# One table for every place of the order in a one-core message-passing kernel, with the steps cut into single products, turns and half runs

## The chip, the cores and the metric

The kernel runs on one core of one Trainium2 chip. The metric is the device time of one execution in microseconds. Three executions of the kernel before took 503.43, 501.66 and 503.40 us, median 503.4.

## The reference

128 graphs of 64 nodes with 128 features get one message layer. For every pair (i, j) of nodes of a graph a two-hidden-layer MLP with layer norms makes a message; the adjacency matrix keeps the messages of real edges alone, and their sum per node goes through a second MLP.

```python
f_i, f_j = broadcast(x, i), broadcast(x, j)                  # (B, N, N, C), B=128, N=64, C=128
h = relu(concat([f_i, f_j], -1) @ msg_w0 + msg_b0); h = layernorm(h)
h = relu(h @ msg_w1 + msg_b1);                      h = layernorm(h)
messages = (h @ msg_w2 + msg_b2) * adj[..., None]
agg = sum(messages, axis=2)
updated = x + mlp(concat([x, agg], -1), upd_w0, ..., upd_b2)  # the same MLP with other weights
```

About one pair in eight is an edge, so the kernel computes messages for edges alone: each graph gets 640 edge slots. (A slow path for graphs with more edges stands at the program's end and is not entered.)

## The kernel before, in words

Two graphs make a pair `p` (64 pairs). Edges are worked on in *chunks* of 512 slots: 4 tiles of 128 edges. Five chunks cover four graphs, and there are 160 chunks. A chunk passes through these steps, each a small function:

- `marks` / `compare` (TensorE `mk`, VectorE `j`) and `node_rows` / `stack` (`i`, and the DMAs on SyncE's queue that put `i` and `j` together in `s`): build one-hot matrices `s` that say which two nodes an edge slot has.
- `gather` (TensorE, into the one PSUM bank `hps`): first layer of the MLP as products of `s` with the nodes' precomputed rows. Rows are kept as a low and a high part, `abl` and `abh`, so each piece of a chunk is a pair of products. Because a graph has 640 slots and a chunk 512, the pieces of five successive chunks are 512; 384+128; 256+256; 384+128; 512 columns wide.
- `relu0` (ScalarE, `h`), `turn_h` (four TensorE transposes by `ident` into the one PSUM bank `hT`), `stats0` (two VectorE statistics of `hT`), and some chunks later `seed` (bias into a `z` bank by ScalarE, or into `u` by GpSimd), `layer1` (four products into one of two banks `z0`, `z1`, from `h` itself), `relu1` (`y`; VectorE for half of the chunks, ScalarE for the others), `stats1`.
- `weights` (GpSimd, `w`) and `reduce` (TensorE, 32-column products into `ys`): the masked sums per node.
- For each block of eight graphs the update MLP: `turn` (transposes), `layer_a`, `layer_b`, `layer_c` (products), `layer_out`, `finish` and the store of `uo`.

A product of two float32 operands stands in the profile as two instructions, a transpose and a gather product as one.

The order on each engine is the order in which the steps are called. Each step is entered with `at(n, place, fn, ...)`: `n` is the chunk step and `place` one of 16 places within a chunk step, worked through in a fixed order; a table `MOVE` shifts single steps to another chunk step, place and rank. The table repeats for every tenth chunk in the steady part (about 29 us), and is written out for the start and the end. `keep_busy(k)` issues products into `ys` that nobody reads: `k` products of 128 columns for k over 4, else `k/2` of 256 columns. The table had moved four of these groups from the start to chunk steps 16 and 20.

Of the kernel before, what the change touches and what calls it, by code (L numbers as in the profile page):

```python
# [23 lines left out]
MOVE = {  # L24
# [335 lines left out]
def tile_gnn(  # L360
# [293 lines left out]
    def edge_path(es):  # L654
# [30 lines left out]
        def zbank(k):  # L685
            return ps_z[k].tile([P, CH * C], F32, name=f"z{k}")


        plan = {}
        early_keys = []  # L690

        def at(n, place, fn, *args):
# [955 lines left out]
```

## Time and profile before

| what | value |
|---|---|
| times of three runs | 501.66, 503.40, 503.43 us |
| span of the profiled execution (its own time, first to last instruction) | 501.7 us |
| busy TensorE products / weight loads | 491.1 us (98%) / 467.9 us (93%) |
| busy VectorE | 460.5 us (92%) |
| busy ScalarE | 397.9 us (79%) |
| busy GpSimd | 353.8 us (71%) |
| granted TensorE clock, mean | 0.998 |
| DMA: moved, share of 16 engines on the main queue | 63.55 MB, 58.7% |

Busy time is the union of an engine's instructions. For TensorE it says little: products are pipelined and their ends are modelled, so two products that overlap in the table may still follow each other slowly or quickly. The pace is read from where instructions *start*. The page's chain of work is empty for this run.

### The profile page before, as it was taken

The page shows a single profiled execution, that of the slowest core. Times are in us where ns is not written, and L with a number is a line of the kernel's source. Part 1 is how long each engine was busy: PE and PEld are TensorE (multiplying, and loading weights), DVE is VectorE, ACT ScalarE, POOL GpSimd, SP SyncE. Part 2 cuts the span into 40 slices and gives each one's busy share as a digit, 9 for nine tenths or more (in the row PEclk, how much of TensorE's full clock was granted, in tenths as well). Part 3 has the DMA queues.
Part 4 walks back from the last instruction along what each step waited for, and adds up shares of the span by engine and source line. Part 5 has one row for each costly group of instructions (what it writes and reads, how often), then busy time and mean ns, then how long its engine had stood idle before and what let it go on. Part 6 is the DMA issues. An engine that isn't in the chain of part 4 may idle for free.

```text
span 501.7 us, 15934 instructions
## 1 busy us (share of the span) xinstructions
PE 491.1 (98%) x5969; PEld 467.9 (93%) x5969; DVE 460.5 (92%) x1225; ACT 397.9 (79%) x907; POOL 353.8 (71%) x563
## 2 busy tenths in 40 slices
PE   8899999999999999999999999999999999999995
PEld 5799999999999999999999999999999999999984
DVE  7899789899999999998999999899999989998885
ACT  6999978889787788978778797877879778867753
POOL 3267686877869687786968768696886679674941
PEclk9999999999999999999999999999999999999999
DMA  4668565566948576684857757475564647345201
GB/s 122 157 138 170 122 129 130 114 133 137 164 104 153 126 141 131 130 161 107 160 128 113 157 121 162 104 171 123 121 154 111 156 107 171 88 113 107 63 23 46
DMA packets 91474, 63.55 MB, mean 127 GB/s; under 512 B 57473, under 2 KB 75522, under 8 KB 91394
## 3 DMA queue, kind: packets, MB, share of 16 engines
q1 hardware_dynamic: 91106, 62.36, 58.7%
q8 instruction: 49, 0.80, 0.7%
q14 instruction: 31, 0.25, 0.2%
q10 hardware_dynamic: 288, 0.13, 0.1%
HBM read 7.15 MB, written 4.19 MB: 23 GB/s over the span
## 4 chain that ended last, share of the span: by engine, by line


## 5 line engine op out<-in xcount | busy, mean ns | idle before, releaser
L1003 PE MATMUL z<-w1c,h 128*128 128x128 f32 x1280 | 167.4, 275 | 0.0
L1003 PEld LDWEIGHTS z<-w1c,h 128*128 128x128 f32 x1280 | 158.1, 192 | 4.1
L613 DVE BATCH_NORM_STATS2 st<-hT 128x6 f32<-128x256 f32 x320 | 120.3, 417 | 21.9 <-PE hT L956 18.7
L951 ACT ACTIVATE h<-hps,b0c 128x512 f32<-128x512 f32 x160 | 109.5, 684 | 24.3 <-PE hps L946 23.0
L993 ACT ACTIVATE z<-b1b,m_sd 128x128 f32<-128x128 f32 x320 | 118.8, 371 | 11.6 <-DVE y L597 4.6
L613 DVE BATCH_NORM_STATS2 st<-y 128x6 f32<-128x256 f32 x320 | 117.9, 417 | 0.1
L989 POOL TENSOR_TENSOR u<-b1b,m_sd 128x512 f32<-128x512 f32 x80 | 82.7, 1042 | 29.8 <-ACT m_sd L621 20.2
L956 PE MATMUL hT<-ident,h 128*128 128x128 f32 x640 | 96.6, 273 | 0.7 <-ACT h L951 0.7
L946 PE MATMUL hps<-s,abl 128*128 128x512 f32 (+3 forms) x256 | 93.4, 370 | 1.0 <-DMA s<-j 0.7
L1045 POOL TENSOR_TENSOR w<-oh,m_q 128x192 f32<-128x192 f16 x126 | 62.5, 509 | 39.9 <-issue 27.1
L956 PEld LDWEIGHTS hT<-ident,h 128*128 128x128 f32 x640 | 74.3, 141 | 1.9 <-ACT h L951 1.0
L946 PE MATMUL hps<-s,abh 128*128 128x512 f32 (+3 forms) x256 | 74.4, 322 | 0.0
L1012 ACT ACTIVATE y<-z 128x512 f32<-128x512 f32 x80 | 47.3, 594 | 30.9 <-PE z L1003 30.8
L928 DVE TENSOR_TENSOR j<-mk,cmpt 128x320 fp32r<-128x320 f32 x124 | 58.3, 470 | 1.4 <-PE mk L920 1.2
L597 DVE CUSTOM_DVE_ANT_0 y<-z,u 128x512 f32<-128x512 f32 x80 | 53.9, 674 | 3.9 <-PE z L1003 2.4
L889 ACT ACTIVATE d<-slot,mid 128x640 f16<-128x640 f16 x64 | 52.7, 826 | 0.7 <-DVE mid L799 0.7
L946 PEld LDWEIGHTS hps<-s,abl 128*128 128x128 f32 x256 | 48.7, 190 | 2.9 <-DMA s<-j 0.9
L946 PEld LDWEIGHTS hps<-s,abh 128*128 128x128 f32 x256 | 48.5, 189 | 0.0
L1060 PE MATMUL ys<-y,w 128*32 128x128 f32 x1488 | 44.3, 274 | 0.0
L1060 PEld LDWEIGHTS ys<-y,w 128*32 128x32 f32 x1488 | 39.7, 110 | 3.6 <-POOL w L1045 2.6
L904 POOL CAST i<-tp 128x640 fp32r<-128x640 f16 x58 | 42.4, 745 | 0.0
L920 PE MATMUL mk<-tp,posall 128*128 128x320 f16 x126 | 38.0, 302 | 0.2 <-DVE j L928 0.2
(195 smaller groups left out, 852.2 us busy)
## 6 DMA issues: line engine op xcount, KB each, us to landing
s<-i SPq DMA_DIRECT2D x124, 160.0 KB, 3.0
s<-j SPq DMA_DIRECT2D x124, 160.0 KB, 2.7
xn<-in_x_dram SPq DMA_DIRECT2D x15, 256.0 KB, 3.8
out_dram<-uo SPq DMA_DIRECT2D x15, 256.0 KB, 2.5
an<-in_adj_dram SPq DMA_DIRECT2D x16, 128.0 KB, 2.8
oh<-tp SPq DMA_TRANSPOSE x64, 3.2
xn<-in_x_dram SPq DMA_DIRECT2D x2, 128.0 KB, 2.8
out_dram<-uo SPq DMA_DIRECT2D x2, 128.0 KB, 3.6
```

Source lines behind the costliest of these rows:

```text
L597: nc.vector._custom_dve(TENSOR_ADD_SAT, out=o, in0=ps, in1=sb, s0=BIG, s1=0.0)
L613: nc.vector.bn_stats(st, src.rearrange("p t c -> p c t"))
L889: nc.scalar.activation(D[p], slot, AF.Abs, bias=blocks[b]["mid"][:, q:q + 1], scale=-1.0)
L928: nc.vector.tensor_tensor(JR[p][:, c], MK.pop((p, k))[:, 0:HC], cmpt[:, c], op=ALU.is_equal)
L946: nc.tensor.matmul(ps[:, c:c + w], lhsT=ab[:, g % 4, :], rhs=s, start=(k == 0), stop=(k == 1))
L951: nc.scalar.activation(H[n], HP.pop(n), AF.Relu, bias=b0c)
L956: nc.tensor.transpose(ps[:, t, :], H[n][:, t * P:(t + 1) * P], ident)
L989: nc.gpsimd.tensor_tensor(U[n], bc(W["b1b"], CH), SR[q][:, k:k + CH].unsqueeze(2).to_broadcast([P, CH, C]), op=ALU.mult)
L993: nc.scalar.activation(z_of(n)[:, t, :], W["b1b"], AF.Copy, scale=SR[q][:, k + t:k + t + 1])
L1003: nc.tensor.matmul(ps[:, t, :], lhsT=h[:, t * P:(t + 1) * P], rhs=W["w1c"], start=added and t == 0, stop=True, skip_group_check=True)
L1045: (nc.vector if p == NP - 2 else nc.gpsimd).tensor_tensor(WT[p][:, g], oh, qs, op=ALU.mult)
L1060: nc.tensor.matmul(YS[b][g * N + m * HN:g * N + (m + 1) * HN, k, :], lhsT=w[:, g, m, u, :], rhs=y, start=(u == 0), stop=(u == TH - 1), til ...
```

## The change

The steps are cut finer, so that each can stand anywhere: `gather` issues one product (piece `j`, part `k`) where it issued all pairs of a chunk; `turn_h` one transpose where it issued four; `layer1` two products; `stats0` and `stats1` one statistic each (half a chunk); the update's `turn` and `layer_*` two of four blocks; `layer_out`'s statistics become steps of their own; `stack` one DMA of two; `seed` one of four tiles. The places and the table `MOVE` are gone. A table `WHEN` gives each step a time in 1/144 of a chunk step, and all steps are sorted by it. Four of the seven groups of `keep_busy` products at the start are no longer entered (7 products of 128 columns, and 1, 1 and 2 of 256 columns). Apart from these, each engine has the same instructions as before, in the same shapes and numbers.

```diff
-MOVE = {
-    "gather@1": (-1, "b", 0), "gather@2": (1, "e", -1), "gather@3": (2, "L0", 4),
...
+SCALE = 144
+WHEN = {
+    "gather.0.0": {0: -178, 1: -188, 2: 76, 3: 267, 4: 227, 5: 127, 6: 5, 7: -110, 8: -233,
...
+        def at(n, tag, fn, *args):
+            v = args[0] if args else 0
+            v = v.b if isinstance(v, Unit) else v
+            t = WHEN.get(f"{fn.__name__}{tag}", {}).get(n % 10 if 14 <= n < 138 else 100 + v, 0)
+            plan.append((SCALE * n + t, len(plan), fn, args))
...
-        def stack(p, half, src):
+        def stack(p, half, g):
...
-        def gather(n):
+        def gather(n, j, k):
-            ps = HP[n] = ps_h.tile([P, CH * P], F32, name="hps")
-            for g, e, c, w in sorted(pieces(n), key=lambda v: -v[3]):
-                s = S[g // 2][:, g % 2, e:e + w]
-                for k, ab in enumerate(blocks[g // (2 * PB)]["ab", g // 4 % 2]):
-                    nc.tensor.matmul(ps[:, c:c + w], lhsT=ab[:, g % 4, :], rhs=s,
-                                     start=(k == 0), stop=(k == 1))
+            if n not in HP:
+                HP[n] = ps_h.tile([P, CH * P], F32, name="hps")
+            g, e, c, w = sorted(pieces(n), key=lambda v: -v[3])[j]
+            nc.tensor.matmul(HP[n][:, c:c + w], lhsT=blocks[g // (2 * PB)]["ab", g // 4 % 2][k][:, g % 4, :],
+                             rhs=S[g // 2][:, g % 2, e:e + w], start=(k == 0), stop=(k == 1))
...
-        def turn_h(n):
+        def turn_h(n, t):
...
-        def layer1(n):
+        def layer1(n, t0):
...
-        early(keep_busy, 7)
-        early(keep_busy, 2)
-        early(keep_busy, 2)
-        early(keep_busy, 4)
...
+        for _, _, fn, args in sorted(plan, key=lambda v: v[:2]):
+            fn(*args)
```

What the table does to the order is seen in the built programs. The first place is TensorE in the steady part, around a chunk of 384+128 columns. Before, the four gather products stand together and the four transposes of the chunk ahead (`hT`) behind them:

```order
L920 MATMUL mk_3638<-tp_3345,posall_141 128x320
L946 MATMUL hps_3642<-s_3270,abl_3094 128x384
L946 MATMUL hps_3642<-s_3270,abh_3095 128x384
L946 MATMUL hps_3642<-s_3270,abl_3094 128x128
L946 MATMUL hps_3642<-s_3270,abh_3095 128x128
L956 MATMUL hT_3647<-ident_132,h_3582 128x128 x4
L1003 MATMUL z0_3667<-w1c_357,h_3196 128x128 x4
```

After, at the same place:

```order
L934 MATMUL hps_3616<-s_3318,abl_3063 128x384
L934 MATMUL hps_3616<-s_3318,abh_3064 128x384
L944 MATMUL hT_3621<-ident_132,h_3514 128x128 x2
L934 MATMUL hps_3616<-s_3318,abl_3063 128x128
L944 MATMUL hT_3621<-ident_132,h_3514 128x128
L934 MATMUL hps_3616<-s_3318,abh_3064 128x128
L944 MATMUL hT_3621<-ident_132,h_3514 128x128
L987 MATMUL z0_3650<-w1c_348,h_3191 128x128 x2
```

Each 128-column gather product now has a transpose right behind it. Over the whole program, of the 128 such products 19 were followed by a transpose before, 64 by another of their own kind, and 45 by a float32 product (`z`, an update layer, an unread one, or one that derives a weight); after, 113 are followed by a transpose, 14 by a `marks` product (`mk`) and 1 by its own kind.

The second place is TensorE some 60 us into the run, where the largest group of unread products stood. Before:

```order
L946 MATMUL hps<-s,abh 128x384
L946 MATMUL hps<-s,abl 128x128
L946 MATMUL hps<-s,abh 128x128
L1326 MATMUL ys<-mean_m 128x128 x7
L1003 MATMUL z_1161<-w1c,h 128x128 x4
L920 LDWEIGHTS posall
L920 MATMUL mk<-tp,posall 128x320
L956 MATMUL hT<-ident,h 128x128 x4
L832 MATMUL ma<-ident,xn 128x128 x4
```

After, the same chunk, up to the same four transposes of `xn`:

```order
L934 MATMUL hps<-s,abh 128x384
L934 MATMUL hps<-s,abl 128x128
L944 MATMUL hT<-ident,h 128x128 x2
L934 MATMUL hps<-s,abh 128x128
L944 MATMUL hT<-ident,h 128x128 x2
L987 MATMUL z_1157<-w1c,h 128x128 x2
L820 MATMUL ma<-ident,xn 128x128 x4
```

The seven unread products are gone, and `hT`'s transposes stand between the gather products.

The third place is TensorE near the end, where the last two update units (half blocks, banks `z_...`) and the block ahead of them (bank `mu`) share the engine. Before:

```order
L1109 MATMUL ma<-ident,uh 128x128 x4
L1123 MATMUL z_9219<-u0a,xnT 128x128
L1123 MATMUL z_9219<-w2u,ysumT 128x128
L1123 MATMUL z_9219<-u0a,xnT 128x128
L1123 MATMUL z_9219<-w2u,ysumT 128x128
L1123 MATMUL mu<-u1c,uhT 128x128 x4
L1109 MATMUL hT<-ident,ysum 128x128 x2
L1109 MATMUL hps<-ident,uh 128x128 x2
L1123 MATMUL z_9262<-u0a,xnT 128x128
```

After:

```order
L1095 MATMUL ma<-ident,uh 128x128 x4
L1112 MATMUL z_9211<-u0a,xnT 128x128
L1112 MATMUL z_9211<-w2u,ysumT 128x128
L1112 MATMUL z_9211<-u0a,xnT 128x128
L1112 MATMUL z_9211<-w2u,ysumT 128x128
L1095 MATMUL hT<-ident,ysum 128x128 x2
L1112 MATMUL mu<-u1c,uhT 128x128 x4
L1095 MATMUL hps<-ident,uh 128x128 x2
L1112 MATMUL z_9248<-u0a,xnT 128x128
```

The last unit's two transposes of `ysum` now stand ahead of the four `mu` products instead of behind them.

More of the change, by code (lines that the diff above doesn't have):

```diff
@@ L1012, in relu1, with stats1 @@
                 nc.scalar.activation(Y[n], ps, AF.Relu)
[L1014 removed]
+        def stats1(n, t):
             q, c = divmod(n, QC)
[L1016 removed]
+            if q not in ST1:
                 ST1[q] = stp.tile([P, QT // 2, 6], F32, name="st1", bufs=2)
[L1018 to L1019 removed]
+            two_stats(ST1[q][:, (CH * c + t) // 2, :], Y[n][:, t:t + 2, :])
         def var1_step(q):
@@ L1104, in residual, with turn @@
                                     op=ALU.add)
-        def turn(u, src):
-            u.ps = u.turns()
-            for q in range(u.n):
+        def turn(u, src, q0):
+            if q0 == 0:
+                u.ps = u.turns()
+            for q in range(q0, q0 + 2):
                 nc.tensor.transpose(u.ps[:, q * P:(q + 1) * P], getattr(u, src)[:, q, :], ident)
@@ L1114, in turn_out, with layer @@
             nc.scalar.copy(getattr(u, src + "T"), u.ps[:, 0:u.n * P])
-        def layer(u, *pairs):
-            ps = u.bank()
-            for q in range(u.n):
+        def layer(u, q0, *pairs):
+            if q0 == 0:
+                u.l = u.bank()
+                u.l_ps = u.l[:, 0:u.n * P].rearrange("p (q c) -> p q c", q=u.n)
+            ps = u.l
+            for q in range(q0, q0 + 2):
                 s = slice(q * P, (q + 1) * P)
@@ L1124, in layer, with layer_a, layer_b, layer_c @@
                                      stop=(n == len(pairs) - 1))
-            u.l_ps = ps[:, 0:u.n * P].rearrange("p (q c) -> p q c", q=u.n)
-        def layer_a(u):
-            layer(u, ("xn", u0a), ("ysumT", W["w2u"]))
-        def layer_b(u):
-            layer(u, ("uhT", W["u1c"]))
-        def layer_c(u):
-            layer(u, ("uyT", W["u2c"]))
+        def layer_a(u, q0):
+            layer(u, q0, ("xn", u0a), ("ysumT", W["w2u"]))
+        def layer_b(u, q0):
+            layer(u, q0, ("uhT", W["u1c"]))
+        def layer_c(u, q0):
+            layer(u, q0, ("uyT", W["u2c"]))
         def layer_out(u, o, bias):
@@ L1193, in edge_path @@
                 (1, 1, 2, 2, 3, 3, 4, 4, 4, 5, 5, 6, 6, 6, 7))
+        for b in range(2):
+            blocks[b]["an"] = an0[b]
+            blocks[b]["xn"] = xn0[b]
         for b in range(NB):
@@ L1241, in edge_path @@
-                at(n + t[6], "a", turn_out, u, "uh")
-                at(n + t[7], "a", upd_root0, u)
+                v = u.tag
+                at(n + m0_at, v, bias0, u)
+                at(n + xo_at, v, residual, u)
+                at(n + t[0], v, sums_out, u)
+                halves = range(0, u.n, 2)
+                for q0 in halves:
+                    at(n + t[1], f"{v}.ysum.{q0}", turn, u, "ysum", q0)
+                at(n + t[2], v + ".ysum", turn_out, u, "ysum")
+                for q0 in halves:
+                    at(n + t[3], f"{v}.{q0}", layer_a, u, q0)
@@ L1243, in edge_path @@
+                at(n + t[4], v + ".uh", layer_out, u, "uh", "m0")
+                for q0 in halves:
+                    at(n + t[4], f"{v}.uh.{q0}", layer_stats, u, "uh", q0)
+                for q0 in halves:
+                    at(n + t[5], f"{v}.uh.{q0}", turn, u, "uh", q0)
+                at(n + t[6], v + ".uh", turn_out, u, "uh")
+                at(n + t[7], v, upd_root0, u)
                 if t is STEADY:
-                    at(n + t[7], "e", upd_shift, u, 0, PB)
+                    at(n + t[7], v, upd_shift, u, 0, PB)
@@ L1255, in edge_path @@
-                at(n + t[13], "x", layer_c, u)
-                at(n + t[14], "e" if b == NB - 3 else "m", finish, u)
+                    for q0 in halves:
+                        at(n + t[7], f"{v}.{q0}", upd_shift, u, q0, q0 + 2)
+                for q0 in halves:
+                    at(n + t[8], f"{v}.{q0}", layer_b, u, q0)
+                at(n + t[9], v + ".uy", layer_out, u, "uy", "usdb")
+                for q0 in halves:
+                    at(n + t[9], f"{v}.uy.{q0}", layer_stats, u, "uy", q0)
@@ L1257, in edge_path @@
+                at(n + t[9], v, upd_m1, u)
+                for q0 in halves:
+                    at(n + t[10], f"{v}.uy.{q0}", turn, u, "uy", q0)
+                at(n + t[11], v + ".uy", turn_out, u, "uy")
+                at(n + t[12], v, upd_root1, u)
+                at(n + t[12], v, upd_inverse, u)
+                for q0 in halves:
+                    at(n + t[13], f"{v}.{q0}", layer_c, u, q0)
+                at(n + t[14], v, finish, u)
         for p in range(NP):
@@ L1260, in edge_path @@
                 if p > 2:
-                    at(max(n - 7, p - 2), "x" if p == PB + 1 else "a", distance, p)
-                    at(max(n - 6, p - 2), "m", make_tp, p)
-                at(n - 5, "x" if p == PB else "a", node_rows, p)
-                at(n - 4, "a", stack, p, 0, IR)
+                    at(max(n - 7, p - 2), "", distance, p)
+                    at(max(n - 6, p - 2), "", make_tp, p)
+                at(n - 5, "", node_rows, p)
+                for g in range(2):
+                    at(n - 4, f".0.{g}", stack, p, 0, g)
                 for k in range(2):
-                    at(n - 5 + k, "k", marks, p, k)
-                    at(n - 5 + k, "k", compare, p, k)
-                at(n - 3, "a", stack, p, 1, JR)
+                    at(n - 5 + k, f".{k}", marks, p, k)
+                    at(n - 5 + k, f".{k}", compare, p, k)
+                for g in range(2):
+                    at(n - 3, f".1.{g}", stack, p, 1, g)
             w = p // 2 * QC + QC + L1 + p % 2
             last = p // 2 == NQ - 1
-            at(w - 4, "a", node_marks, p)
+            at(w - 4, "", node_marks, p)
             q, h = divmod(p, 2)
@@ L1284, in edge_path @@
             end = q * QC + QC + L1
-            at(3 if q == 0 else n, "s" if last else "x" if q == 0 else "e0", var0_of, q)
-            at(*((n, "e0") if last else (n + 1, "b")), root_of, q)
-            at(end - last, "e1", var1_step, q)
+            at(n if last else n + 1, "", root_of, q)
+            at(end - last, "", var1_step, q)
             wait = 0 if last else 2
-            at(end + wait, "x" if q == NQ - 2 else "a", root1_of, q)
-            at(end + wait, "x" if q == NQ - 2 else "m", inverse_of, q)
+            at(end + wait, "", root1_of, q)
+            at(end + wait, "", inverse_of, q)
         def by_vector(n):
@@ L1370, in edge_path @@
-        early(place_rest)
-        early(rows, 0, 0, 0, 2)
-        early(keep_busy, 4)
-        early(rows_hi, 0, 0, 0, 2)
-        early(rows_lo, 0, 0, 0, 2)
-        early(marks_here, 0)
-        early(rows, 0, 0, 2, 4)
-        early(keep_busy, 2)
-        early(rows_here, 0, 0)
-        early(rows_here, 0, 1)
-        early(compare_here, 0, 0)
-        early(distance, 1)
-        early(gather, 0)
-        early(relu0, 0)
-        early(keep_busy, 4)
-        early(compare_here, 0, 1)
-        early(make_tp, 1)
@@ new lines, in edge_path @@
+        early(".0", degrees, 0)
+        early("", place_first)
+        early(".0", distance, 0)
+        early(".0", place_pair, 0)
+        early(".0", make_tp, 0)
+        early("", place_rest)
+        early(".0.0.0.2", rows, 0, 0, 0, 2)
+        early(".3", keep_busy, 4)
+        early(".0.0.0.2", rows_hi, 0, 0, 0, 2)
+        early(".0.0.0.2", rows_lo, 0, 0, 0, 2)
+        early(".0", marks_here, 0)
+        early(".0.0.2.4", rows, 0, 0, 2, 4)
+        early(".0.0", rows_here, 0, 0)
+        early(".0.1", rows_here, 0, 1)
@@ new lines, in edge_path @@
+        early(".0.0", compare_here, 0, 0)
+        early(".1", distance, 1)
+        early(".0.0.0", gather, 0, 0, 0)
+        early(".0.0.1", gather, 0, 0, 1)
+        early(".0", relu0, 0)
+        early(".5", keep_busy, 4)
+        early(".0.1", compare_here, 0, 1)
+        early(".1", make_tp, 1)
+        early(".2", distance, 2)
+        early(".1", marks_here, 1)
+        early(".1.0.0", gather, 1, 0, 0)
+        early(".1.0.1", gather, 1, 0, 1)
+        early(".1.1.0", gather, 1, 1, 0)
+        early(".1.1.1", gather, 1, 1, 1)
@@ new lines, in edge_path @@
+        early(".1", relu0, 1)
+        early(".0.0.2.4", rows_hi, 0, 0, 2, 4)
+        early(".1.0", rows_here, 1, 0)
+        early(".1.1", rows_here, 1, 1)
+        early(".1.0", compare_here, 1, 0)
+        early(".0.0.2.4", rows_lo, 0, 0, 2, 4)
+        early(".2.0.0", gather, 2, 0, 0)
+        early(".2.0.1", gather, 2, 0, 1)
+        early(".2.1.0", gather, 2, 1, 0)
+        early(".2.1.1", gather, 2, 1, 1)
+        early(".2", relu0, 2)
+        early(".7", keep_busy, 2)
+        early(".2", make_tp, 2)
@@ L1420, in keep, with empties @@
                 product(W["ps", k])
-            at(n - 1, "x", ahead)
-            at(n, "x", keep)
-            at(n + 1, "m", lambda k=k, empty=empty: empty(W.pop(("ps", k))))
+            def empties(k=k, empty=empty):
+                empty(W.pop(("ps", k)))
+            at(n - 1, f".{k}", ahead)
+            at(n, f".{k}", keep)
+            at(n + 1, f".{k}", empties)
         for n, k in ((2, 2), (3, 2), (4, 2), (5, 2)):
-            at(n, "e", keep_busy, k)
+            at(n, f".n{n}", keep_busy, k)
         fl = const.tile([P, 3], F32, name="fl")
```

406 lines of the change are left out of this document (233 added, 173 removed), and 543 rows, old and new, of tables (MOVE, WHEN).

## The prediction

> **What bounds the kernel now.** I read the page's busy times first, then the busy times by windows, the timelines of TensorE's weight loads and products, the waits, and the DMA issues. The page's first row:
>
> ```profile
> PE 491.1 (98%) x5969; PEld 467.9 (93%) x5969; DVE 460.5 (92%) x1225; ACT 397.9 (79%) x907; POOL 353.8 (71%) x563
> ```
>
> TensorE looks like the bound, VectorE is close behind. The windows (busy time of PE, PEld, DVE, ACT, POOL, granted clock, DMA share, GB/s) say where:
>
> ```profile
> 30.00:40.00 10.00, 10.00 (x108) 9.36 (x107) 9.93 (x24) 9.77 (x27) 6.87 (x11) 1.00 0.83 169
> 48.00:55.00 7.00, 7.00 (x56) 6.64 (x54) 5.92 (x18) 6.77 (x17) 2.89 (x5) 1.00 0.42 97
> 55.00:62.00 7.00, 7.00 (x58) 6.79 (x58) 5.43 (x15) 6.21 (x17) 4.58 (x12) 1.00 0.65 143
> 220.00:225.00 5.00, 5.00 (x44) 4.89 (x43) 5.00 (x14) 3.51 (x9) 3.65 (x5) 1.00 0.58 125
> 250.00:300.00 50.00, 50.00 (x546) 48.77 (x545) 47.34 (x127) 41.02 (x96) 37.11 (x59) 1.00 0.64 130
> 475.00:502.00 27.00, 20.16 (x270) 18.09 (x268) 17.54 (x50) 12.73 (x38) 8.26 (x17) 0.97 0.11 32
> ```
>
> From 30 us on TensorE never pauses; the granted clock is 1.00. VectorE has 2.66 of 50 us free in the steady part, but in places (220 to 225 us) nothing, and in the stretch from 30 to 40 us VectorE and ScalarE are both full. So TensorE sets the time while the order keeps VectorE just inside it. Only from 475 us does TensorE stand idle for long, with a dependent chain of update work.
>
> Busy time does not show TensorE's pace, so I take it from the starts of weight loads (start, length, then the group). A load can run while the product ahead still streams, so I only use distances over whole stretches.
>
> ```profile
> 101.81 0.47 PEld L956 LDWEIGHTS hT<-ident,h 128*128 128x128 f32 x4
> 102.25 0.97 PEld L1003 LDWEIGHTS z<-w1c,h 128*128 128x128 f32 x8
> 103.14 0.19 PEld L946 LDWEIGHTS hps<-s,abl 128*128 128x128 f32 x1
> ...
> 70.69 0.19 PEld L946 LDWEIGHTS hps<-s,abl 128*128 128x128 f32 x1
> 70.86 0.19 PEld L946 LDWEIGHTS hps<-s,abh 128*128 128x128 f32 x1
> 71.00 0.42 PEld L956 LDWEIGHTS hT<-ident,h 128*128 128x128 f32 x4
> 71.38 0.30 PEld L1003 LDWEIGHTS z<-w1c,h 128*128 128x128 f32 x2
> ...
> 105.54 0.19 PEld L946 LDWEIGHTS hps<-s,abh 128*128 128x128 f32 x1
> 105.65 0.30 PEld L1123 LDWEIGHTS mu<-u0a,xnT 128*128 128x128 f32 x2
> 105.87 0.30 PEld L1123 LDWEIGHTS mu<-w2u,ysumT 128*128 128x128 f32 x2
> ```
>
> The first three rows are the scale: a transpose takes (102.25−101.81)/4 = 0.110 us, a record of a float32 product (103.14−102.25)/8 = 0.111. In both lower blocks the `abl`, `abh` named last before the other kind are the 128-column pair. A product's own time shows between the next load and the one after it. With transposes behind the pair, 70.86 to 71.38 is `abl`, `abh` and three transposes: 0.52−0.33 = 0.19 us for the pair. Of this `abl`, with its own kind behind it, has 70.86 to 71.00, 0.14; so `abh`, with a transpose behind it, has 0.05 to 0.06. With float32 products behind the pair, 105.54 to 105.87 is the pair and one record: 0.33−0.11 = 0.22, that is 0.11 each. So a 128-column gather product is short when a transpose follows it and long otherwise.
>
> **The change part by part.** Instructions and shapes are the same apart from the unread products; everything else is place.
>
> *128-column gather products.* The order has 19 pairs whose second product a transpose follows and 45 with a float32 product behind them: 45×0.22+19×0.19 = 13.5 us. After, nearly every product has a transpose behind it; I take 2×0.06 = 0.12 a pair, 64×0.12 = 7.7. That saves 5.8 us. About 59 of the 64 pairs lie after the first 62 us, where TensorE is never idle, and I take 5.3. Bounds: if splitting the pair leaves 0.19 each, 64×0.19 = 12.2 and 1.3 us is saved; if the price does not depend on the neighbour, 0; 5.8 at most.
>
> The Trainium skill, page "TensorE: Matmul & The Clock Gate", section "LDWEIGHTS (loading the stationary operand)", speaks against this term: it gives a load's time as its number of columns divided by 1.2 per ns, the same for every 128-column load, which by estimate is 107 ns. By that, a 128-column product can cost no less than its successor's load, whatever the successor is, and the term would be 0. The transposes and float32 records at 0.11 agree with it, the 0.05 to 0.06 above does not; so I go by the rows and keep the rule's result as a rival.
>
> *Unread products.* The four groups of `keep_busy` that fall out, and what follows each:
>
> ```profile
> 48.73 1.08 PE L1329 MATMUL ys<-first,mean_m 128*128 128x256 f32 x4
> 49.65 0.60 PE L956 MATMUL hT<-ident,h 128*128 128x128 f32 x4
> 50.08 0.60 PE L1329 MATMUL ys<-first,mean_m 128*128 128x256 f32 x2
> 50.52 1.05 PE L1003 MATMUL z<-w1c,h 128*128 128x128 f32 x8
> ...
> 53.87 0.65 PE L1329 MATMUL ys<-first,mean_m 128*128 128x256 f32 x2
> 54.35 0.60 PE L956 MATMUL hT<-ident,h 128*128 128x128 f32 x4
> ...
> 60.31 1.77 PE L1326 MATMUL ys<-mean_m 128*128 128x128 f32 x14
> 61.92 0.50 PE L1003 MATMUL z<-w1c,h 128*128 128x128 f32 x3
> ```
>
> By starts they hold TensorE 0.92+0.44+0.48+1.61 = 3.45 us. Upper bound 3.45. Lower bound 0, since they could stand where TensorE would wait anyway: in 48 to 55 us ScalarE is busy 6.77 of 7.00, so of the three small groups' 1.84 us I take a third, 0.6. In 55 to 62 us VectorE has 1.57 and ScalarE 0.79 us free, and the `z` product behind the last group waits for a bank that ScalarE seeds just before:
>
> ```profile
> 59.11 1.17 ACT L993 ACTIVATE z<-b1b,m_sd 128x128 f32<-128x128 f32 x3
> ```
>
> That bank is ready at 60.3, when the group starts, so the product could have followed at once: I take all 1.6. Sum 2.2, range 0 to 3.45. If the cover is gone, what is late next is `relu0` and the seeds on ScalarE.
>
> *256-column products and the rest of the steady order.* Products followed by their own kind go from 96 to 55 in the order, by float32 products from 0 to 57, by transposes from 30 to 15. Spacing of loads puts 256 columns at about 0.124 us in the first two cases and less with a transpose; so 15 fewer short and 41 fewer own-kind successors nearly cancel. I take 0.4, between a loss of 0.5 and a gain of 1.0, the largest I get by letting the 41 save 0.024 each. The `layer1` halves, `q` and `marks` products keep their prices: 0.
>
> *The transfers.* `stack`'s DMAs now go out one by one on SP's queue, `i` and `j` alternating in halves, ahead of or behind an `xn` load.
>
> ```profile
> PE hps L946 <- DMA s<-j: 0.7, 1, 0.7
> ...
> s<-i SPq DMA_DIRECT2D x124, 160.0 KB, 3.0
> s<-j SPq DMA_DIRECT2D x124, 160.0 KB, 2.7
> ```
>
> Over the whole span TensorE waits once, 0.7 us, for `s`; the transfers land in 3.0 and 2.7 us, about one chunk's time (29.3 us for ten chunks). Cost 0; if that cover goes, one late transfer costs up to 3.0 us, once. I put it in the range only.
>
> *The tail.* The last unit's `ysum` transposes move ahead of four `mu` products:
>
> ```profile
> 487.09 0.35 ACT L1091 COPY ysum<-ys 128x256 f32<-128x256 f32 x1
> 488.32 1.10 PE L1123 MATMUL mu<-u1c,uhT 128*128 128x128 f32 x8
> 489.26 0.38 PE L1109 MATMUL hT<-ident,ysum 128*128 128x128 f32 x2
> 489.70 0.39 PE L1123 MATMUL z<-u0a,xnT 128*128 128x128 f32 x2
> 490.11 0.49 PE L1123 MATMUL z<-w2u,ysumT 128*128 128x128 f32 x2
> ```
>
> `ysum` was ready at 487.44, so the transposes gain 489.26−488.32 = 0.94 us. But the `hps` transposes of `uh` and the product with `xnT` stay behind `mu`; what can be gained is the delay of the product with `ysumT`, 490.11 against 489.70+0.22: 0.2 us, and a little more if ScalarE's copy is better placed. I take 0.3, range 0 to 0.94.
>
> *What is given back.* In the steady part TensorE gains some 5.7 us of 440, 1.3%. VectorE has 5% free on average and none in places, and the one bank `hT` hands work from TensorE to it:
>
> ```profile
> DVE st L613 <- PE hT L956: 18.7, 43, 1.6
> ACT y L1012 <- PE z L1003: 30.8, 44, 1.3
> ```
>
> These waits, 18.7 and 30.8 us in all, are TensorE being the later one; they shrink as it gets faster. They add to more than the gain, so I give back only 0.5 us, range 0 to 4 (half of the gain and more; the second rival).
>
> Sum: 2.2+5.3+0.4+0.3−0.5 = 7.7 us. The profiled execution's span is 501.7, its own time, as the fastest of the three runs (501.66); the other two and the median are 1.7 above it, and nothing in the profile says why. 501.7−7.7 = 494.0 for an execution like the profiled one, 495.7 for one like the others. I predict 495.0, one us of the 1.7 above the sum, and add the same to the cases below.
>
> **The rivals.**
>
> *Slower: spread transposes starve VectorE.* Before, four transposes of a chunk follow each other in 0.44 us. After, gather products, and sometimes `z` products, stand between them, so the last of four comes some 0.5 us later after the first (at the place of the diff's second order, two gather products and their neighbours). VectorE's statistics run in order: a late `hT` holds up everything behind it there (`j`, `y`), and those hold TensorE. VectorE has 2.66 us per 50, 0.156 us per chunk of 2.93 us, to spare, and the gain is 7.7/160 = 0.048 us per chunk. So from 0.20 us of new wait per chunk the kernel is slower; with half of the 0.5 us exposed, 0.25, it loses (0.25−0.156)×160 = 15 us: 501.7+15−7.7+1 = 510. For it: one `hT` bank, 43 waits already. Against it: the statistics are halved as well, so the first half can start after two transposes.
>
> *The cover runs out.* TensorE gets shorter, but VectorE, full in 220 to 225 and in 30 to 40 us, and ScalarE at the start do not; they give back half of the 8.2 that TensorE saves by the terms above: 501.7−4.1+1 = 498.6. For it: the full windows. Against it: the free 5% is four times the gain.
>
> *The price of a 128-column product does not change.* The saving at a transpose is then only a matter of when the load is recorded, and the 5.3 falls out: 501.7−2.4+1 = 500.3. That is also the time that the skill's rule would give. For it: the loads' starts need not be the products' starts. Against it: the lower blocks above compare whole stretches, 0.52 and 0.33 us, and differ.
>
> *More than that.* A new order of every place can also take out idle time at both ends, where TensorE stands 6.8 us in the tail window; with 3.45 for the unread products and 4 us of that: 501.7−(3.45+5.8+0.4+4)+1 = 489.0. For it: idle time is there. Against it: at the end the chain of one unit's steps is as long as before.
>
> **How the numbers follow.** The forecast (gain of 5 to 11 us) has 0.62, the run-out cover 0.17, the unchanged price 0.08, the slower rival 0.07, the further gain 0.06. About 0.5% (2.5 us) is what can be told from no change: faster is below 500.9. The forecast and the further gain are all faster, 0.68; of the run-out cover 0.14, with 0.03 no change; the unchanged price sits 0.6 us inside, so 0.04 each: faster 0.86, no change 0.07, slower 0.07. The forecast's own range is 491 to 498. The range reaches down to 489.5, just short of the further gain, and over the cover and price cases to 500.5, leaving out the slower rival and the edges of both others, about 0.15.
>
> **What the changed kernel's profile would show.** PE records fall from 5969 to about 5947 and no unread products stand after 45 us. The load behind a 128-column gather product followed by a transpose comes about 0.06 us after the one before; at 0.11 the pair term is wrong. Ten chunks take about 28.9 us in place of 29.3. VectorE's busy time stays near 460 us and its share of a 50 us window rises from 47.3 to about 48; VectorE's waits for `hT` fall below 18.7 us (the slower rival: they rise, and TensorE waits for VectorE's `j` or for `hT`'s statistics). PE shows no new waits for `s`. In 48 to 62 us TensorE stays at 14 of 14 busy; a gap there says that the unread products had covered a wait. I am wrong if single banks tie the spread steps more tightly than the waits of before show.

## The result and the profile after

The changed kernel took 535.6 us (median of four runs, 535.2 to 535.9), the kernel before 502.75 us beside it: a ratio of 1.0653, with a 95% interval of 1.0628 to 1.0677. It is 33 us slower, where 495.0 was forecast. The profiled execution spans 533.6 us.

The page's first row and two windows of the changed kernel (PE, PEld, DVE, ACT, POOL busy, granted clock, DMA share, GB/s):

```profile
PE 502.1 (94%) x5947; PEld 461.3 (86%) x5947; DVE 465.2 (87%) x1225; ACT 396.9 (74%) x907; POOL 350.1 (66%) x563
...
48.00:62.00 14.00, 13.31 (x102) 11.51 (x100) 12.05 (x34) 11.60 (x30) 8.18 (x17) 1.00 0.60 139
250.00:300.00 50.00, 47.50 (x630) 44.31 (x630) 44.44 (x116) 37.23 (x82) 35.76 (x54) 1.00 0.60 139
```

TensorE, which never paused in 250 to 300 us before, now stands still for 2.50 of 50 us, and VectorE went from 47.34 to 44.44: no engine is full any more. The work is the same apart from the unread products, so the engines wait for each other. The waits of the changed kernel (engine and line, what it waited for, total us, times, longest us) say where; the last row is what my slower rival would have had to show:

```profile
ACT z L981 <- PE z L987: 36.2, 44, 2.1
PEld z L987 <- ACT z L981: 35.2, 58, 1.3
...
PE z L987 <- ACT z L981: 16.0, 27, 1.0
...
DVE st L630 <- PE hT L944: 20.1, 40, 2.1
```

ScalarE's seeds of a `z` bank wait 36.2 us for TensorE's products in `z`, and TensorE's weight loads wait 35.2 us for the seeds. Before, the waits list has neither: no seed that waits for TensorE and no load or product that waits for a seed. One such place, from the timeline:

```profile
277.38 0.61 PE L987 MATMUL z<-w1c,h 128*128 128x128 f32 x4
277.71 0.47 PEld L944 LDWEIGHTS hT<-ident,h 128*128 128x128 f32 x4
277.82 0.60 PE L944 MATMUL hT<-ident,h 128*128 128x128 f32 x4
278.08 0.37 ACT L981 ACTIVATE z<-b1b,m_sd 128x128 f32<-128x128 f32 x1 [0.60 <-PE z L987]
278.50 0.52 PEld L987 LDWEIGHTS z<-w1c,h 128*128 128x128 f32 x4 [0.32 <-ACT z L981]
278.51 0.71 PE L987 MATMUL z<-w1c,h 128*128 128x128 f32 x4
```

A half of `layer1` runs in a `z` bank; a seed tile of the *same chunk*, meant for the second half, stands behind it in the order and waits until it is done (0.60 us, ended by PE `z`); then the second half waits for that seed. I call this a turn of the bank: it goes from TensorE to ScalarE and back. The tiles are different ones of the bank, but the built program has these waits all the same. The Trainium skill, page "PSUM — Partial Sum Buffer", section "PSUM bank collisions raise a hardware error", tells why: two engines on one bank in the same partitions at once collide even in disjoint columns, so access is guarded by bank and not by address. That these waits are there, the rows show; what would happen without them no run here shows.

The table has it so in three of every ten chunks. In its unit (144 a chunk step) chunk 2 of ten has seed tiles at 695, 709, 710 and **900** with the halves of `layer1` at 794 and 917; chunk 0 has its last seed at 924 between 918 and 926; chunk 4 two seeds at 843 and 850 between 840 and 1065. Before, `layer1` was one step behind all seeds.

A fourth wait in ten chunks is no turn. Here are the other three places of one such stretch (the fourth is the load at 278.50 above), with ScalarE's seeds at the first:

```profile
250.68 0.78 ACT L981 ACTIVATE z<-b1b,m_sd 128x128 f32<-128x128 f32 x2 [0.80 <-PE z L987]
...
251.50 0.52 PEld L987 LDWEIGHTS z<-w1c,h 128*128 128x128 f32 x4 [0.34 <-ACT z L981]
...
253.83 0.52 PEld L987 LDWEIGHTS z<-w1c,h 128*128 128x128 f32 x4 [1.35 <-ACT z L981]
...
273.80 0.30 PEld L987 LDWEIGHTS z<-w1c,h 128*128 128x128 f32 x2 [0.49 <-ACT z L981]
```

By the order of the table, the loads at 251.50, 273.80 and 278.50 are the second halves of chunks 4, 0 and 2 of ten, behind their turns: 0.34+0.49+0.32 = 1.15 us. The longest wait, 1.35 us at 253.83, is the first half of chunk 5. All seeds of its chunk stand ahead of it, and it waits for all four of them though it needs two. Together the four waits are 2.50 us.

To see where the loss lies I take ScalarE's `h` instructions as milestones: one for each chunk, 160 in both kernels. These are those of chunks 80 and 90, counted from 0, before and then after:

```profile
234.97 0.69 ACT L951 ACTIVATE h<-hps,b0c 128x512 f32<-128x512 f32 x1
...
264.41 0.69 ACT L951 ACTIVATE h<-hps,b0c 128x512 f32<-128x512 f32 x1
```

```profile
248.44 0.69 ACT L939 ACTIVATE h<-hps,b0c 128x512 f32<-128x512 f32 x1
...
280.29 0.69 ACT L939 ACTIVATE h<-hps,b0c 128x512 f32<-128x512 f32 x1
```

From chunk 40 to 120, ten chunks take 29.43 us before and 31.84 after, in every stretch within 0.03 us: 2.41 us more, close to the four waits. Chunk 20 is 1.0 us later, chunk 130 25.5 us, the last one 35.2 us, and 3.3 us come back behind it: 31.9 us between the two spans.

### The profile page after: what moved, and what is told of

Same layout as the page of the kernel before. It is cut to its first block, busy times and chain, and to the rows that moved or that the text cites. A ratio compares the mean times of both kernels' runs of the same rounds, so it can differ in the third digit from the quotient of the medians.

```text
span 533.6 us, 15954 instructions
## 1 busy us (share of the span) xinstructions
PE 502.1 (94%) x5947; PEld 461.3 (86%) x5947; DVE 465.2 (87%) x1225; ACT 396.9 (74%) x907; POOL 350.1 (66%) x563
## 4 chain that ended last, share of the span: by engine, by line
## 5 line engine op out<-in xcount | busy, mean ns | idle before, releaser
L987 PE MATMUL z<-w1c,h 128*128 128x128 f32 x1280 | 200.8, 281 | 19.2 <-ACT z L981 16.0
L987 PEld LDWEIGHTS z<-w1c,h 128*128 128x128 f32 x1280 | 173.9, 191 | 41.7 <-ACT z L981 35.2
L981 ACT ACTIVATE z<-b1b,m_sd 128x128 f32<-128x128 f32 x320 | 118.5, 371 | 43.7 <-PE z L987 36.2
L630 DVE BATCH_NORM_STATS2 st<-hT 128x6 f32<-128x256 f32 x320 | 121.7, 418 | 21.2 <-PE hT L944 20.1
L630 DVE BATCH_NORM_STATS2 st<-y 128x6 f32<-128x256 f32 x320 | 123.6, 415 | 0.9 <-ACT y L998 0.8
L944 PE MATMUL hT<-ident,h 128*128 128x128 f32 x640 | 112.5, 278 | 3.0 <-DVE st L630 2.8
L934 PE MATMUL hps<-s,abl 128*128 128x512 f32 (+3 forms) x256 | 98.0, 386 | 0.6 <-ACT h L939 0.5
L934 PE MATMUL hps<-s,abh 128*128 128x512 f32 (+3 forms) x256 | 89.9, 355 | 0.0
L944 PEld LDWEIGHTS hT<-ident,h 128*128 128x128 f32 x640 | 76.4, 141 | 6.3 <-DVE st L630 4.2
L1030 POOL TENSOR_TENSOR w<-oh,m_q 128x192 f32<-128x192 f16 x126 | 64.6, 525 | 18.4 <-DVE m_q L659 14.8
L877 ACT ACTIVATE d<-slot,mid 128x640 f16<-128x640 f16 x64 | 51.0, 818 | 1.0 <-POOL mid L766 0.6
L648 POOL TENSOR_TENSOR m_v<-m_v,st 128x20 f32<-128x20 f32 x31 | 7.2, 231 | 58.6 <-DVE st L630 58.3
```

The costliest lines, as they stand in the source:

```text
L630: nc.vector.bn_stats(st, src.rearrange("p t c -> p c t"))
L877: nc.scalar.activation(D[p], slot, AF.Abs, bias=blocks[b]["mid"][:, q:q + 1], scale=-1.0)
L934: nc.tensor.matmul(HP[n][:, c:c + w], lhsT=blocks[g // (2 * PB)]["ab", g // 4 % 2][k][:, g % 4, :], rhs=S[g // 2][:, g % 2, e:e + w], star ...
L944: nc.tensor.transpose(HT[n][:, t, :], H[n][:, t * P:(t + 1) * P], ident)
L981: nc.scalar.activation(z_of(n)[:, t, :], W["b1b"], AF.Copy, scale=SR[q][:, k:k + 1])
L987: nc.tensor.matmul(ps[:, t, :], lhsT=H[n][:, t * P:(t + 1) * P], rhs=W["w1c"], start=by_vector(n) and t == 0, stop=True, skip_group_check= ...
```

## The experiments

| run | us | ratio to before (95%) | us per ten chunks, 40 to 120 |
|---|---|---|---|
| changed kernel | 535.6 | 1.065 (1.063 to 1.068) | 31.84 |
| e1_seeds_first | 521.3 | 1.037 (1.035 to 1.039) | 30.70 |
| e2_layer1_late | 520.1 | 1.034 (1.033 to 1.036) | 30.64 |
| e3_before_split | 528.1 | 1.050 (1.049 to 1.052) | 31.78 |
| e4_turns_together | 535.9 | 1.066 (1.064 to 1.067) | 31.89 |
| e5_layer1_whole | 517.0 | 1.027 (1.024 to 1.030) | 30.25 |
| e6_pairs_together | 517.8 | 1.029 (1.026 to 1.032) | 30.37 |
| e7_before_no_unread | 501.4 | 0.998 (0.996 to 0.999) | 29.49 |
| e8_late_and_one_whole | 516.7 | 1.026 (1.024 to 1.028) | 30.28 |
| e10_early_and_one_whole | 520.7 | 1.034 (1.032 to 1.036) | 30.61 |
| e3b_before_one_split | 511.4 | 1.018 (1.014 to 1.021) | 30.24 |
| e11_two_whole | 511.4 | 1.016 (1.012 to 1.020) | 29.91 |
| e12_pairs_on_e11 | 512.2 | 1.017 (1.013 to 1.021) | 29.99 |
| e13_tail_whole | 512.6 | 1.019 (1.015 to 1.023) | 29.91 |

The diffs below show the main lines of each change; what a name stands for is said in a comment.

**Is it the turn in the bank?** Two runs take it out of the changed kernel, one by ScalarE's order and one by TensorE's; one puts it into the kernel before; one undoes the rival's cause.

```diff
+        half = {args[0]: t for t, _, fn, args in plan if fn is layer1 and args[1] == 0}
+        plan = [(min(t, half[args[0]] - 1) if fn is seed else t, k, fn, args)   # e1
+                for t, k, fn, args in plan]
```

> The changed kernel, with every tile of a seed placed ahead of its chunk's first layer1 half (only ScalarE's order changes). Theory (a seed tile placed between the two halves of layer1 makes TensorE, ScalarE and TensorE take turns in one z bank, three times in ten chunks): ten chunks fall from 31.85 us to 29.0 to 29.6, the time to 502 to 509 us. Rival (spread transposes starve VectorE): stays within 3 us of 535.6, ten chunks near 31.8.

```diff
+        plan = [(max(t, seeded[args[0]] + 1)       # e2; seeded: time of the chunk's last seed
+                 if fn is layer1 and args[0] in seeded else t, k, fn, args) for t, k, fn, args in plan]
```

> The changed kernel, with the first layer1 half placed behind the chunk's last seed tile (only TensorE's order changes). Theory (turns in one z bank): as when the seeds are moved, ten chunks 29.0 to 29.8 us, 502 to 511 us. If instead ScalarE's order as such costs the time, little comes back: over 525 us. Rival (spread transposes): over 530 us.

```diff
             for t in range(CH):                    # e3, layer1 of the kernel before
+                if t == 2 and 20 <= n < 128 and n % 10 in (0, 2, 4):
+                    seed(n, 3)                     # left out of the seeds ahead
```

> The kernel before, with the last seed tile placed between the two halves of layer1 in the chunks 0, 2 and 4 of every ten from 20 to 127; all else as before. Theory (turns in one z bank, 2.4 us per ten chunks, 33 chunks): 512 to 530 us, ten chunks 30.3 to 31.9 us. Rival (spread transposes): within 3 us of 502.7.

```diff
+        plan = [(turned[args[0]] if fn is turn_h   # e4; turned: time of the chunk's last turn_h
+                 else max(t, turned[args[0]] + 1) if fn is stats0 else t, k, fn, args)
+                for t, k, fn, args in plan]
```

> The changed kernel, with the four transposes of each chunk put together at the place of the last. Theory (turns in one z bank): 533 to 541 us, since the bank's turns stay and the short products behind which a transpose stood are lost. Rival (spread transposes starve VectorE): at most 512 us, and VectorE's waits for hT fall below 18 us.

The turn alone, put into the kernel before in 33 chunks, makes it 25.3 us slower and its ten chunks 31.78 us, as slow as the changed kernel's. Its waits:

```profile
PEld z L1009 <- ACT z L998: 23.1, 33, 1.0
...
PE z L1009 <- ACT z L998: 16.8, 33, 0.8
```

33 waits for 33 turns, 0.70 us of stopped weight loads for each. The rival falls: with the transposes together the time stays (535.9), and VectorE's wait for `hT` is 23.7 us, not less. But removing the turns gave back 14.3 and 15.5 us, not the 25 to 34 expected, and in ten chunks 1.14 and 1.20 us. That is about what TensorE waited behind the three turns of the changed kernel, 1.15 us. So the turn costs time by itself, but in the changed kernel it is half of the loss; that e3_before_split comes out as slow as the changed kernel is a coincidence of sizes. In e3 nothing stands between the two halves and each turn costs its full length, while in the changed kernel other products fill a part of it.

> The kernel before with one turn in a z bank in ten chunks (chunk 2 of ten) in place of three. If each turn has its price by itself: a third of the 25.3 us that three cost, 6 to 11 us more than before. If one turn is absorbed by slack on the other engines and only several together cost: under 3 us.

```diff
-                if t == 2 and 20 <= n < 128 and n % 10 in (0, 2, 4):
+                if t == 2 and 20 <= n < 128 and n % 10 == 2:
```

One turn in ten chunks costs 8.1 us, three 25.3: 0.74 and 0.77 us a turn (11 and 33 turns). Within the spread of the runs they add up, and no slack takes any of it.

**What comes behind it.** With `layer1` late (e2), the loads still wait twice in ten chunks for seeds: 0.90 us for those of chunk 4 and 0.49 us for those of chunk 5.

```diff
+        plan = [(half[args[0]] if fn is layer1 else t, k, fn, args)   # e5; half: time of the later half
+                for t, k, fn, args in plan]
```

> The changed kernel, with both halves of every layer1 together at the place of the later half (TensorE's order alone changes). Theory: with the halves apart, the earlier half stands up to one and a half chunk steps ahead, and TensorE waits there for seeds that ScalarE can't have done yet; together, that wait goes too, and ten chunks fall from 30.7 (seeds ahead of layer1) to 29.2 to 29.6 us, the time to 500 to 508 us. Rival (ScalarE is full in that stretch wherever layer1 stands): ten chunks stay above 30.3 us, 516 to 522 us.

The time, 517.0 us, lies where the rival had it (516 to 522), and the ten chunks, 30.25, just below its 30.3. But the rival's cause is not the one: no wait for seeds is left in the steady part. Other chunks' later `layer1` makes VectorE late in turn, and TensorE waits twice in ten chunks, ahead of `hT` transposes, for VectorE's statistics of the chunk before, as here:

```profile
269.18 0.74 DVE L630 BATCH_NORM_STATS2 st<-hT 128x6 f32<-128x256 f32 x2
...
270.07 0.63 PE L944 MATMUL hT<-ident,h 128*128 128x128 f32 x4 [0.31 <-DVE st L630]
```

So only the chunks with the wait are moved:

```diff
+        late.update({args[0]: t for t, _, fn, args in plan        # e8, on top of e2
+                     if fn is layer1 and args[1] == 2 and args[0] % 10 == 4 and 14 <= args[0] < 128})
```

> The changed kernel with layer1's first half behind the chunk's last seed tile, and in chunks 4 of every ten (halves 1.5 chunk steps apart) both halves together at the later place; the other chunks' halves stay apart. Theory (the steady loss is the z banks' turns in chunks 0, 2 and 4, and the new VectorE waits of the run with whole layer1 came from moving the other chunks' halves): ten chunks 29.1 to 29.6 us, 503 to 508 us. Rival (VectorE's statistics of hT set the pace once the turns are gone): ten chunks stay at 30.2 or more, 515 us or more.

> As the run before, with the seeds of chunks 0 and 2 moved ahead of layer1 in place of layer1 behind them. Theory: the same, 29.1 to 29.7 us per ten chunks, 503 to 509 us. Rival: 30.2 us or more, 515 us or more.

 (its edit is that of e1, with chunk 4's halves together)

Neither theory holds: 30.28 and 30.61 us per ten chunks, 516.7 and 520.7 us, all in the range of the rival. But in the ten chunks of e8 TensorE nowhere waits for VectorE's statistics, as the rival would have it. A single long wait of TensorE is left, for the seeds of chunk 5, which follow the root of a whole group's statistics:

```profile
241.39 0.30 ACT L638 ACTIVATE m_sd<-st,eps_c 128x20 f32<-128x20 f32 x1
241.73 0.78 ACT L981 ACTIVATE z<-b1b,m_sd 128x128 f32<-128x128 f32 x2
242.44 0.67 ACT L939 ACTIVATE h<-hps,b0c 128x512 f32<-128x512 f32 x1
243.01 0.76 ACT L981 ACTIVATE z<-b1b,m_sd 128x128 f32<-128x128 f32 x2
243.83 0.71 PE L987 MATMUL z<-w1c,h 128*128 128x128 f32 x4 [0.59 <-ACT z L981]
```

The two last seed tiles stand behind `relu0`, and the first half of `layer1`, which needs neither, waits for both: the turn's mirror image, with the whole bank waited for again. It is the place of the longest wait of the changed kernel.

```diff
-                     if fn is layer1 and args[1] == 2 and args[0] % 10 == 4 and 14 <= args[0] < 128})
+                     if fn is layer1 and args[1] == 2 and args[0] % 10 in (4, 5) and 14 <= args[0] < 128})
```

> As the run with layer1 late and one chunk's halves together, and the halves of chunk 5 of every ten together at the later place too. That run's trace has one long wait of TensorE left in ten chunks, 0.75 us and 0.10 behind it, for the seeds of chunk 5. If that place is the only one left: ten chunks 29.2 to 29.6 us, 503 to 508 us. If ScalarE and VectorE as a whole are late and the wait only moves on: 30.0 us or more, 513 us or more.

Now 511.4 us and 29.91 per ten chunks, between the two expectations, and TensorE is full again (as the window shows), but the kernel before needs 29.43:

```profile
250.00:300.00 50.00, 49.95 (x540) 47.98 (x539) 47.87 (x125) 40.78 (x94) 36.85 (x60) 1.00 0.58 131
...
240.81 0.19 PEld L934 LDWEIGHTS hps<-s,abl 128*128 128x128 f32 x1 [0.22 <-ACT h L939]
...
241.78 0.14 PEld L944 LDWEIGHTS hT<-ident,h 128*128 128x128 f32 x1 [0.21 <-issue]
```

Two short waits of the loads, 0.22 and 0.21 us, which the kernel before does not have, add up to nearly the 0.48 that remains. That they are its cause is not shown, nor why the issue is late there.

```diff
-                     ... args[0] % 10 in (4, 5) and 14 <= args[0] < 128})
+                     ... (args[0] % 10 in (4, 5) and args[0] >= 14 or args[0] >= 128)})
```

> As the run with two chunks' halves together, and from chunk 128 to the end every layer1 whole at the later half's place. Of that run's 8 us over the kernel before, 6 to 7 arise from chunk 130 to the last relu0, with 1.5 us of TensorE's waits for seeds and 2.5 for hT among them. If the waits for seeds there are the same mechanism and stand alone: 1 to 3 us faster than that run, 508 to 510 us. If VectorE's statistics are late there in any order: no faster, 511 us or more.

No gain (512.6 against 511.4): the loss at the end is not the early half's. That VectorE's statistics are late there, as the second expectation had it, fits and is not shown.

**The two terms of the prediction.**

```diff
+        plan = [(low[args[0]] if fn is gather and args[1:] == (1, 1) and args[0] % 5 in (1, 3)  # low: gather 1, 0
+                 else t, k, fn, args) for t, k, fn, args in plan]
```

> The run with whole layer1, and in addition the second 128-column gather product directly behind the first, where a transpose stood between. If a 128-column product is short with a transpose behind it, net of what the transpose ahead of it loses (0.25 us per ten chunks), this costs 2 to 5 us against the run with whole layer1. If the price doesn't depend on the neighbour: within 1 us of it.

> The run before this one, and in addition the second 128-column gather product directly behind the first, where a transpose stood between. Loads of the earlier pair of runs put the price at 0.20 us of TensorE per ten chunks, 0.41 for the products less 0.21 that the transposes get back: 2 to 4 us slower than the run before this one if TensorE sets the pace there; within 1 us of it if a wait still does.

0.8 us each by the medians, 0.12 and 0.08 per ten chunks. On the kernel with waits left this proved little; on e11, where TensorE is full, it does. The weight loads of the same chunk, first e11, then e12 with the pair together:

```profile
248.64 0.20 PEld L934 LDWEIGHTS hps<-s,abl 128*128 128x128 f32 x1
248.79 0.19 PEld L934 LDWEIGHTS hps<-s,abh 128*128 128x128 f32 x1
248.97 0.32 PEld L944 LDWEIGHTS hT<-ident,h 128*128 128x128 f32 x2
249.26 0.19 PEld L934 LDWEIGHTS hps<-s,abl 128*128 128x128 f32 x1
249.39 0.14 PEld L944 LDWEIGHTS hT<-ident,h 128*128 128x128 f32 x1
249.43 0.21 PEld L934 LDWEIGHTS hps<-s,abh 128*128 128x128 f32 x1
249.59 0.14 PEld L944 LDWEIGHTS hT<-ident,h 128*128 128x128 f32 x1
249.62 0.55 PEld L987 LDWEIGHTS z<-w1c,h 128*128 128x128 f32 x4
250.09 0.25 PEld L1095 LDWEIGHTS ma<-ident,ysum 128*128 128x128 f32 x2
```

```profile
249.57 0.20 PEld L934 LDWEIGHTS hps<-s,abl 128*128 128x128 f32 x1
249.72 0.19 PEld L934 LDWEIGHTS hps<-s,abh 128*128 128x128 f32 x1
249.90 0.32 PEld L944 LDWEIGHTS hT<-ident,h 128*128 128x128 f32 x2
250.18 0.19 PEld L934 LDWEIGHTS hps<-s,abl 128*128 128x128 f32 x1
250.29 0.19 PEld L934 LDWEIGHTS hps<-s,abh 128*128 128x128 f32 x1
250.43 0.20 PEld L944 LDWEIGHTS hT<-ident,h 128*128 128x128 f32 x2
250.60 0.53 PEld L987 LDWEIGHTS z<-w1c,h 128*128 128x128 f32 x4
251.04 0.25 PEld L1095 LDWEIGHTS ma<-ident,ysum 128*128 128x128 f32 x2
```

In e11 the load two behind each 128-column product does come early (249.39 to 249.43 and 249.59 to 249.62, 0.04 us or less; 0.06 was predicted), but the distances around it are longer than 0.11: 0.13 ahead of the first (249.26 to 249.39) and 0.16 between the two (249.43 to 249.59). From the first `abl` to `ma` both hold the same products: 250.09−248.64 = 1.45 and 251.04−249.57 = 1.47 us. The time had moved to the neighbours.

```diff
-        early(keep_busy, 7)      # and likewise the groups 2, 2 and 4 that the change leaves out
+        early(keep_busy, 0)
```

> The kernel before without the four groups of unread products that the change leaves out; nothing else is moved. If they cost what the prediction took, 2.2 us less (500.6); bounds 0 (other engines set the pace there, 502.8) and 3.45 us less (499.4). Slower than before only if the products kept something else in step.

1.5 us less by the medians (0.4 to 2.0 by the ratio's interval). In the trace 0.8 us of the 3.45 come out between chunks 10 and 30, around the places of the groups; the rest went into new waits. (1.3 us more of the difference between the two traces arise before chunk 10, ahead of the groups, and have another source.) From 46 to 60 us TensorE is no longer full:

```profile
46.00:60.00 14.00, 13.03 (x103) 12.05 (x102) 11.42 (x32) 13.08 (x32) 7.48 (x15) 1.00 0.50 115
```

This is the one version faster than the kernel before, by 0.2%, with an interval that ends 0.1% short of no change.

## Why the prediction was wrong

- **The bound** was read rightly: TensorE sets the pace, and the order keeps the others just inside it. I then costed the change by TensorE's own stretches, and took the order of the others as given.
- **The step that failed** is the sentence "The `layer1` halves, `q` and `marks` products keep their prices: 0." The halves' own time did not change, but with a step in halves another engine's step of the same bank comes between, or the early half comes before the bank is ready. In the changed kernel the loads wait 2.50 us per ten chunks for seeds, where 2.41 were lost: 1.15 behind the three turns, and 1.35 at chunk 5, whose first half waits for seeds of the second. With the turns taken out ten chunks go from 31.84 to 30.64, with chunk 4's halves together to 30.28, and with chunk 5's to 29.91. "What is given back", 0.5 us and at most 4, is the term that should have held this. It was to be seen beforehand, in the table and in the order of ScalarE, where a seed follows its own chunk's product. I looked at TensorE's order alone. The prediction's last sign of being wrong, single banks that tie the spread steps more tightly than the waits of before show, is what came.
- **128-column products, 5.3 us:** mis-sized. Between them together and apart lie 0.08 us per ten chunks, about 1 us. The short distance was real, but I took a distance of two loads for a product's cost, and the rival, a price that does not change, was nearer. The rule that I had set beside it, of the Trainium skill, page "TensorE: Matmul & The Clock Gate", section "LDWEIGHTS (loading the stationary operand)", has a load's time go by its columns alone. Over the closed stretch above the trace agrees with it (1.45 against 1.47 us); single distances, from 0.04 to 0.16 us, do not. My lower bound with the pair split, 1.3 us, was near. The price of a pair with a float32 product behind it, 0.22 us, on which that bound rests too, was not tested by a run of its own.
- **Unread products, 2.2 us:** 1.5 by the times, 0.8 in the trace; inside the range, and the cover did run out as the range's lower end supposed. "In 48 to 62 us TensorE stays at 14 of 14 busy" was wrong: 13.31, and 13.03 of 14 in 46 to 60 us when only these products go.
- **256-column products, 0.4 us:** not measured alone. From each one's next load to the one after, the eight of ten chunks take 0.95 us before and in e11, so nothing; but this is the kind of price that misled me for the 128-column products.
- **Transfers, 0:** right. No wait of TensorE for `s` stands among the changed kernel's.
- **The tail, 0.3 us:** the small step is right: the product with `ysumT` now starts 0.23 us behind the one with `xnT`, which before took 0.41.

```profile
520.95 0.38 PE L1095 MATMUL hT<-ident,ysum 128*128 128x128 f32 x2
521.17 1.06 PE L1112 MATMUL mu<-u1c,uhT 128*128 128x128 f32 x8
...
522.28 0.39 PE L1112 MATMUL z<-u0a,xnT 128*128 128x128 f32 x2
522.51 0.39 PE L1112 MATMUL z<-w2u,ysumT 128*128 128x128 f32 x2
```

  It drowns in the last thirty chunks, whose loss (35.2 less 25.5 us, of which the turns are a part) I had not looked for.
- **The slower rival** had the right kind of cause, one bank handed between two engines, and the wrong bank. I gave it 0.07 for `hT` and never asked it of `z`, where the split was. VectorE's waits for `hT`, 20.1 against 18.7 us, hardly moved, e4_turns_together gained nothing, and from 200 to 325 us TensorE never waits for VectorE in the changed kernel: `hT` is not the cause there.
- **The base, 501.7 us:** I took the profiled execution for one like the fastest of three. In every execution here whose span is on record the time is 1.7 to 1.9 us above the span, so a span of 501.7 belongs to the runs of 503.4. This moves the sum to 495.7, 0.7 us above the forecast, and explains nothing of the loss. The "29.3 us" of ten chunks is 29.43 by the milestones.

**Still open:** 0.48 us per ten chunks of e11 and some 6 us from chunk 130 on. They were not traced to one cause. The single DMAs of `stack` and the halved statistics were not undone in a run of their own.

## What to carry to other kernels

When a step is split, list for each buffer who writes it in between: a bank that two engines write was handed over here at each change of hand, even between disjoint tiles, and an early half waited for tiles that it did not need. Read the order of every engine that shares a bank with a moved step, and keep "all seeds, then all products" as one unit. A price per instruction that is read from starts has to hold over a stretch with the same content at both ends, or it only moves time from one row to the next.

## What the runs showed of the hardware

One change of hands TensorE to ScalarE to TensorE, with no other product in between, costs TensorE 0.74 to 0.77 us here (e3b and e3). One of e3:

```profile
249.83 0.50 PE L1009 MATMUL z<-w1c,h 128*128 128x128 f32 x3
...
250.43 1.87 ACT L998 ACTIVATE z<-b1b,m_sd 128x128 f32<-128x128 f32 x5 [0.56 <-PE z L1009]
...
250.85 0.71 PE L1009 MATMUL z<-w1c,h 128*128 128x128 f32 x4 [0.52 <-ACT z L998]
```

It is 0.10 us from the products' end (249.83+0.50) to the seed, 0.37 us of seed (the first of the five in 1.87 us; the others are of another bank), 0.05 us to the next product, and the four records then take 0.71 in place of the 0.61 us of four that follow without a wait. That is 0.62 us. The rest, some 0.16 us by estimate, is the length of the last product (0.28) less the 0.11 after which the next one would have started. Such turns add up within the spread of the runs (11 for 8.1 us, 33 for 25.3), where TensorE has no slack to take them.

The spread of the runs before (501.66 to 503.43) may have a source ahead of the first chunk: these are the first `h` of the kernel before and of e7, whose engines do the same work up to there, 1.0 us apart. Two traces can't show that this is the spread, nor what makes it.

```profile
12.32 0.69 ACT L951 ACTIVATE h<-hps,b0c 128x512 f32<-128x512 f32 x1
...
11.32 0.69 ACT L951 ACTIVATE h<-hps,b0c 128x512 f32<-128x512 f32 x1
```
